# A graph layer with mixer and mixture of experts: a fifth node taken by maxima over all rows, a last slice of 123 steps, later scatters, and the last experts' weights issued behind the last fold

## The chip, the cores and the metric

The kernel runs on one core of one Trainium2 chip. The time is the device time of one execution in microseconds; the time of the kernel before is the median of three runs. One further execution was recorded by the hardware profiler, and every duration below is from that record. Differences of about 0.2% (2.4 us) are the smallest that these runs can tell from none.

## The reference

Cut to what matters here: `x` has 3125 rows (nodes, tokens) of 256 numbers, and there are 100000 edges `src -> dst`, sorted by `dst`, most of them into the lowest nodes.

```python
xn = layernorm(x)
# graph part: for each edge relu((xn[dst]-xn[src]) @ theta.T + xn[src] @ phi.T), maximum over the edges of a node
x = x + segment_max(relu(...), dst) + mixer(xn)          # a node without edges gets 0
xt = x; probs = softmax(layernorm(xt) @ Wr + br); top_p, top_idx = top_k(probs, 2)
h = gelu(einsum('end,edh->enh', xe, W1) + b1)            # 8 experts, 256 -> 1024 -> 256
x = x + sum over the two picked experts of weight * (h @ W2 + b2)
```

What an edge adds splits into a part of its source, `b = xn @ (phi - theta).T`, and a part of its destination; so a node needs only the maximum of `b` over its sources.

## The kernel before, in words

The nodes make 25 tiles of 128. The edges lie in reversed order of their destination over 128 partitions with 782 steps each: one step is one indirect gather on GpSimd (POOL, L107) that brings 128 rows of `b_d` into a window buffer (pool "g", five buffers of eight rows per partition), and one VectorE instruction `fold` (L366) that carries the running maximum along. Windows are stored to `s_d` through the SP queue (`move(nc.sync, ...)` in `folding`); the row at which a node's run ends is gathered from there again (`r`).

The steps are cut into four slices (`STEPS`), each of which completes a group of node tiles (`GROUPS`): tiles 12 to 24, then 5 to 11, then 1 to 4, then tile 0. When a slice is folded, its group follows: `carry` (L373 to L389) joins the partitions' maxima, `token_tile` (L425 on) makes the tokens and the router's logits, `dispatch` scatters the tokens' rows to `xs_d` by expert (POOL, L114), and `Stream.go` runs the experts over the rows in lots: load of rows, transposes (L698), scale `xe` (L709), first matmuls `hp` (L615), gelu (L617), second matmuls `yp` (L639), bias (L753), store to `ys_d`. An expert's 2 MB of weights come in four parts of 512 KB on ScalarE's DMA queue. Tile 0 is done by `dense_tile`: it goes through all eight experts in the order `DENSE` (5, 6, 7, 0, 1, 2, 3, 4) without routing, each with its own scaled input `xe` (L802, VectorE); three experts' weights are left from the stream, two (0 and 1) come in 1 MB halves by `dense_half`, three by `next_dense`. `combine` gathers the two expert rows of every token of the other tiles (POOL), weighs them on VectorE (L1308) and stores them to `out` (SP); it uses the window buffers.

The last 27 steps (`REST`) are never gathered. They hold edges into the nodes below `FIRST` = 4. For these `first_nodes` counts by one-hot matmuls which rows have an edge into which node and makes a mask `no_edge`, and `first_maxima` takes the maximum of all of `b` plus mask: 25 tiles times four nodes of VectorE instructions (L1228), spread at one per 1.4 ticks, then transposes (L1235), a reduction, two more transposes (L1242) and the result `first`, which tile 0 needs at L440. The last `KEPT` = 6 steps of slice 3 aren't stored: `pick_ends` (L1287) takes the ends in them from SBUF by one-hot matmuls that `last_ends` prepares.

The order of PE, VectorE, ScalarE and SP is written out by hand. Pieces of work are generators with a due time in ticks; a tick is one gather on POOL (about 1.25 us). `yield 8` in such a piece says that what follows is issued no earlier than 8 ticks on, and every engine's stream has just the order in which the pieces issued.

Of the kernel before, what the change touches and what calls it, by code (L numbers as in the profile page):

```python
# [8 lines left out]
F32 = mybir.dt.float32  # L9
# [5 lines left out]
OP = mybir.AluOpType  # L15
# [23 lines left out]


GROUPS = ((12, 25), (5, 12), (1, 5), (0, 1))
STEPS = (240, 195, 194, 126)
CAPS = (512, 256, 176)
LOT = (256, 256, 176)
G = len(GROUPS)
COL = [sum(STEPS[:g]) for g in range(G + 1)]


FIRST = 4
REST = T - COL[G]  # L50
W = 8
WN = 5
# [15 lines left out]
def gps_layer(ctx: ExitStack, tc: tile.TileContext, x, src, dst, thetaT, phiT, gbias, wq, wkvT,  # L68
# [583 lines left out]
    class Stream:  # L652
# [67 lines left out]
        def go(self):  # L720
            units = Units(self.ps, self.act)
            u, q = 0, -1
            for k in range(3):
                self.next_w(k)
                yield 25
            while True:
                if u == len(self.lots):

                    for _ in units.last():
                        yield room()  # L730
                    units.behind = None
                    if not self.open:
                        break
                    if G - 3 in self.through:
                        nc.scalar.activation(table, eps, AF.Sqrt)
                    while u == len(self.lots):
                        yield 1
                if ("xe", u) not in self.held:
                    self.rows(u // 2)
                    yield 8  # L740
                    self.turn(u)
                    yield 2
                    self.scaled(u)
                    yield 2
                g, e, h = self.lots[u]
                v = u // 2
                if u % 2 == 0:
                    ys = self.at(2) if v % 2 else self.act.tile([P, 4, D], F32, name="ys", bufs=1)

                def done(r, yp, u=u, ys=ys):  # L750
                    g, e, h = self.lots[u]
                    n = self.half(u)
                    nc.tensor.matmul(yp[0:n, :], ident[0:E, e:e + 1].to_broadcast([E, n]), b2_sb, start=False, stop=True)  # L753
                    nc.scalar.copy(ys[0:n, u % 2 * 2 + r, :], yp[0:n, :])
                    if u % 2 and r:
                        move(nc.scalar, self.two(ys_d, u // 2), self.as_two(ys, u // 2))
                        if u + 1 == len(self.lots) or self.lots[u + 1][0] != g:
                            self.through.add(g)

                between = {4: lambda: self.turn(u + 1), 6: lambda: self.scaled(u + 1)}  # L760
                if u % 2 == 0:
                    between[1] = lambda: self.rows(v + 1)
                if h == 0:
                    q += 1
                    if q:
                        between[7] = lambda: (self.next_w(q + 2, self.parts), self.part())
                at_step = dict(between)
                for f in (0, 2, 5):
                    between[f] = lambda f=f: (self.part(), at_step.get(f, int)())
                w1t, w2t = self.held["w", q]  # L770
                for _ in units.run(e, w1t, self.held["xe", u], w2t, done, between, 2, self.half(u)):
                    yield room()
                u += 1
            for k in range(3):
                dense_w[DENSE[k]] = self.held["w", q - 2 + k]
            dense_half(0, 1, xn_hi[:, 0:FC, :].rearrange("p i d -> p (i d)"), nc.scalar)
            clock["through"] = True

    def spread(pool, i, pick):
# [6 lines left out]
    def dense_tile(act, ps, mm, i, shared, w, next_w, order=range(E), ready=None):  # L786
# [5 lines left out]
        xT = act.tile([P, 2, P], F32, name="xT", bufs=1)  # L792
        nc.vector.tensor_copy(xT, tr)
        held = {}
        yield 1

        def scaled(k):
            if k < E:
                e = order[k]
                held["xe", e] = act.tile([P, 2, ROWS], F32, name="xe")  # L800
                for c in range(2):
                    nc.vector.tensor_scalar(held["xe", e][:, c, 0:P], xT[:, c, :], sm[:, c, e:e + 1],  # L802
                                            sm[:, 2 + c, e:e + 1], op0=OP.mult, op1=OP.add)

        while ready is not None and "through" not in ready:
            yield 1
        scaled(0)
        o = act.tile([P, D], F32, name="o", bufs=1)

        def second_bias():  # L810
# [156 lines left out]
    def first_nodes():  # L967
# [8 lines left out]
        nc.vector.tensor_scalar(high, high, lane, None, op0=OP.subtract)  # L976
        yield 1
        counts = no_edge.rearrange("p k i -> p (k i)")
        some = 7
        for t0 in range(0, REST, some):  # L980
            n = min(some, REST - t0)
            ones_of = []
# [125 lines left out]
    def dispatch(g, half, i0, i1, top, top_i, taken):  # L1108

        ro = at_hand["route"]  # L1110
        while not all(i in routed for i in range(i0, i1)) or len(taken) < half:
            yield 1
        yield 1
        made = []
        at = i0 - GROUPS[g][0]
        rest = shares(ro, i0, i1, top[:, at:at + i1 - i0, :], top_i[:, at:at + i1 - i0, :], made,
                      15 if g == G - 2 and half == 0 else 0)
        start(rest, clock["now"] + next(rest))
        yield from slots(ro, mm, g, half, i0, i1, made[0], taken)
        yield 1 if g == G - 2 else 9  # L1120
        put = []
        for i in range(i0, i1):
            n = rows_in(i)
            for k in range(2):
                put.append((xs_d[g][:], slot_i[0:n, k, i:i + 1], xn2(i)[0:n]))
        scatter(*put)

    def group(g):
# [42 lines left out]
            start(first_maxima())  # L1171
        if g == G - 2:
            clock["routed"] = True
            start(verdict())

    odd = keep.tile([1, 1], I32, name="odd")
# [30 lines left out]
    def first_maxima():  # L1207
# [11 lines left out]
        for i in range(NT):  # L1219
# [4 lines left out]
            for k in range(FIRST):  # L1224
# [4 lines left out]
                                                   op1=OP.max)  # L1229
                yield 1.4  # L1230
        most = at_hand["first"].tile([P, 2, FIRST], F32, name="most")
        for c in range(2):
            tr = mm.tile([P, FIRST, P], F32, name="mm")
            for k in range(FIRST):
                nc.tensor.transpose(tr[:, k, :], of_k[:, k, c * P:(c + 1) * P], ident)  # L1235
            on_pe(1.2)
            yield 4
            nc.vector.tensor_reduce(most[:, c, :], tr, AX.X, OP.max)
            yield 2
        rows_p = mm.tile([FIRST, 2, P], F32, name="mm")  # L1240
        for c in range(2):
            nc.tensor.transpose(rows_p[:, c, :], most[:, c, :], ident)  # L1242
# [2 lines left out]
        ends["first"] = at_hand["first"].tile([FIRST, D], F32, name="first")  # L1245
        nc.vector.tensor_copy(ends["first"], rows_p.rearrange("k c p -> k (c p)"))

        dense_half(0, 0, xn_lo[:, 1:1 + FC, :].rearrange("p i d -> p (i d)"))
        yield from last_ends()

    def end_ones(j):
        return xn_lo[:, SPLIT - KEPT // 2:SPLIT, :].rearrange("p i (c k) -> p (i c) k", k=P)[:, j, :]

    def last_ends():

# [59 lines left out]
    def combines(g):  # L1315

        i0, i1 = GROUPS[g]
        whole = i1 - (i1 == NT)
        for i in range(i0, whole, W // 2):
            nt = min(W // 2, whole - i)  # L1320
            start(combine(g, i, nt))
            yield 2 * nt
            if g == 0 and i == i0 + W // 2:

                while "shared" not in clock:
                    yield 1
                yield 6
                for k in range(2):
                    dense_half(1, k, wide.tile([P, HALF], F32, name="g"))
        if i1 == NT:  # L1330
            start(combine(g, NT - 1, 1))
            yield 2

    def finale():

        for g in range(G - 1):
            while g not in at_hand["ffn"].through:
                yield 1
            yield from combines(g)

    def starts(g):

# [7 lines left out]
    def folding():  # L1350

        for g in range(G):
            last = None
            rows = s_d[1 + P * COL[g]:1 + P * COL[g + 1], :].rearrange("(p t) d -> p t d", t=STEPS[g])
            for w, (t0, n) in enumerate(starts(g)):
# [6 lines left out]
                if g < G - 1 or t0 + n < STEPS[g]:  # L1362
                    move(nc.sync, rows[:, t0:t0 + n, :], wins[g, w][:, 0:n, :])
            clock["last"] = last
            if g == 0:
                open_late()
            start(group(g))
# [193 lines left out]
```

## Time and profile before

| | us |
|---|---|
| median of three runs (lowest, highest) | 1219.15 (1218.51, 1221.02) |
| the profiled execution | 1217.85 |
| its span, first to last instruction | 1216.0 |
| busy: TensorE, VectorE, ScalarE, POOL | 938.2, 678.6, 326.0, 885.8 |
| experts of group 0 on TensorE | 528 to 794 |
| experts of group 1 | 802 to 939.5 |
| experts of group 2 | 1007.8 to 1140.3 |
| last gather of an edge step (POOL) | 1114.62 |
| dense tile: first hp to the last o | 1140.36 to 1208.95 |

The mean granted TensorE clock of this execution is 0.856 of full speed. In the lines of the profile a row names the engine, the source line, the operation with the program's names (`out<-in`) and, in brackets, the engine's idle time before it with what ended it. In the table of stretches each row gives the busy time and the number of instructions of every engine, then the granted TensorE clock, the busy share of the DMA engines and the GB/s that they moved. In the chain of work that ended last, each row is a start, a duration and what ran or was waited for.

### The profile page before, as it was taken

The numbers are of one execution on the slowest core, as the hardware profiler recorded it, in microseconds if no ns is written. First come the engines' busy times: TensorE is split into PE (matmuls) and PEld (weight loads), VectorE is DVE, ScalarE is ACT, GpSimd is POOL, SyncE is SP. The second block draws the span as 40 slices with busy tenths as digits, with TensorE's granted clock in tenths as the row PEclk, the third lists the DMA queues.
The fourth block names the chain that finished last, engine by engine and source line by source line (L and its number), as shares of the span: only waits on it lengthen the run. The fifth ranks groups of instructions, "written<-read, shape, count | busy, mean of one in ns | idle before, by whom it ended". The sixth has DMA issues, their size and how long they took to land.

```text
span 1216.0 us, 13364 instructions
## 1 busy us (share of the span) xinstructions
PE 938.2 (77%) x3929; PEld 670.4 (55%) x3929; DVE 678.6 (56%) x1998; ACT 326.0 (27%) x762; POOL 885.8 (73%) x911
## 2 busy tenths in 40 slices
PE   6556866645923548689999999979999527999986
PEld 5323433323311323258888887868887315777786
DVE  7669866685336772433333587455546764433633
ACT  4212222210101222133333343323332112332331
POOL 6677777777777777777777777777777777776733
PEclk9778888866965557889999999989999557999998
DMA  8668877666685664467888787689999658998683
GB/s 280 214 200 277 302 253 242 227 227 207 207 292 194 239 235 157 156 238 258 285 307 310 251 284 271 227 308 356 380 370 367 219 191 305 375 387 301 201 338 94
DMA packets 103928, 320.13 MB, mean 263 GB/s; under 512 B 20897, under 2 KB 44186, under 8 KB 92325
## 3 DMA queue, kind: packets, MB, share of 16 engines
q0 software_dynamic: 44032, 119.73, 31.5%
q1 hardware_dynamic: 29724, 115.08, 24.4%
q10 hardware_dynamic: 30089, 84.36, 19.3%
q8 instruction: 33, 0.54, 0.2%
q14 instruction: 50, 0.41, 0.1%
HBM read 192.05 MB, written 127.04 MB: 262 GB/s over the span
## 4 chain that ended last, share of the span: by engine, by line
PE 43%; DMA 5%; issue 4%; POOL 3%; DVE 2%; ACT 1%; ACTq 0%; POOLq 0%; DVEq 0%; SPq 0%
PE yp L639 18%; PE hp L615 18%; PE yp L753 3%; POOL g L107 2%; DMA w<-in_w 2%; DMA g<-b_d,srcI 2%; PE trf L698 1%; POOL xs_d L114 1%; DMA xn_lo<-b_d 1%; PE am L445 1%; DVE g L366 1%; PE mm L491 0%; DMA xn_hi<-xs_d 0%; DMA r<-s_d,end_i 0%; PE mm L403 0%
## 5 line engine op out<-in xcount | busy, mean ns | idle before, releaser
L107 POOL DMA_INDIRECT g<-b_d,srcI x755 | 738.2, 978 | 238.4 <-issue 203.8
L366 DVE SCALAR_TENSOR_TENSOR g<-g,cut 128x256 f32<-128x256 f32 x751 | 363.5, 484 | 356.8 <-DMA g<-b_d,srcI 339.0
L639 PE MATMUL yp<-w,hT 128*128 128x256 f32 (+1 forms) x1120 | 296.8, 387 | 0.0
L615 PE MATMUL hp<-xe,w 128*128 128x256 f32 (+2 forms) x1216 | 285.9, 361 | 11.5 <-issue 5.6
L615 PEld LDWEIGHTS hp<-xe,w 128*128 128x128 f32 x1216 | 216.7, 196 | 49.2 <-issue 18.0
L617 ACT ACTIVATE hT<-hp,sm 128x256 f32<-128x256 f32 (+2 forms) x320 | 140.2, 439 | 335.8 <-PE hp L615 335.3
L639 PEld LDWEIGHTS yp<-w,hT 128*128 128x128 f32 (+1 forms) x1120 | 201.1, 185 | 39.7 <-issue 12.4
L1012 PE MATMUL kv<-wkv,xn_lo 128*128 128x512 f32 x96 | 54.5, 720 | 38.0 <-DVE kn L1030 24.1
L1012 PE MATMUL kv<-wkv,xn_hi 128*128 128x512 f32 x104 | 59.3, 724 | 30.9 <-DVE kn L1030 30.2
L107 POOL DMA_INDIRECT g<-ys_d,from_i x48 | 46.1, 960 | 32.4 <-DVE g L1308 18.7
L445 PE MATMUL am<-cr,oh 128*128 128x257 f32 x86 | 37.3, 560 | 27.8 <-DVE r L450 19.9
L1012 PEld LDWEIGHTS kv<-wkv,xn_lo 128*128 128x128 f32 x96 | 21.1, 231 | 63.8 <-issue 60.3
L1012 PEld LDWEIGHTS kv<-wkv,xn_hi 128*128 128x128 f32 x104 | 22.8, 230 | 58.3 <-issue 55.6
L1228 DVE SCALAR_TENSOR_TENSOR xn_lo<-xn_lo,no_edge 128x256 f32<-128x256 f32 x96 | 45.9, 479 | 16.1 <-DMA xn_lo<-b_d 16.1
L401 PE MATMUL mm<-bias,ones 1*128 1x512 f32 x50 | 32.4, 731 | 16.2 <-ACT x_sb L408 12.9
L753 PE MATMUL yp<-b_sb,ident 8*128 8x256 f32 (+1 forms) x128 | 43.9, 422 | 0.0
L1016 ACT ACTIVATE sq<-kv 128x1024 f32<-128x1024 f32 x25 | 25.5, 1019 | 59.3 <-PE kv L1012 59.3
L445 PEld LDWEIGHTS am<-cr,oh 128*128 128x128 f32 x86 | 20.3, 267 | 37.1 <-issue 24.9
L709 ACT ACTIVATE xe<-trf,sm 128x256 f32<-128x256 f32 (+1 forms) x64 | 31.3, 544 | 27.6 <-PE trf L698 27.6
L1035 PEld LDWEIGHTS dots_p<-kn,vn 128*128 128x128 f32 x200 | 26.9, 199 | 19.0 <-issue 19.0
L1024 ACT ACTIVATE rsk<-var,eps 128x16 f32<-128x16 f32 x25 | 7.7, 308 | 110.7 <-DVE var L1021 110.7
L698 PE MATMUL trf<-ident,xn_hi 128*128 128x128 f32 (+1 forms) x128 | 19.2, 275 | 22.2 <-DMA xn_hi<-xs_d 22.2
(285 smaller groups left out, 991.1 us busy)
## 6 DMA issues: line engine op xcount, KB each, us to landing
s_d<-g SPq DMA_DIRECT2D x80, 1024.0 KB
w<-in_w ACTq DMA_DIRECT2D x84, 512.0 KB
w<-in_w ACTq DMA_DIRECT2D x6, 2048.0 KB
g<-b_d,srcI POOLq DMA_INDIRECT x755, 4.5
s_d<-g SPq DMA_DIRECT2D x13, 896.0 KB
xn_hi<-xs_d ACTq DMA_DIRECT2D x12, 512.0 KB
xs_d<-zero ACTq DMA_DIRECT2D x8, 512.0 KB
b_d<-bt SPq DMA_DIRECT2D x5, 640.0 KB
```

The lines of the kernel that those rows point to most:

```text
L107: got = nc.gpsimd.indirect_dma_start(out=to, out_offset=None, in_=table, in_offset=row_index(index))
L366: nc.vector.scalar_tensor_tensor(g[:, j, :], last, cut[:, t:t + 1], g[:, j, :], op0=OP.add, op1=OP.max)
L401: nc.tensor.matmul(am, ones[0:1, :], bias, start=True, stop=False)
L445: nc.tensor.matmul(r2, picks[k], carried[g], start=(k == 0), stop=(k == len(slices) - 1))
L615: nc.tensor.matmul(hp[:, 0:n], w1t[:, c, f, :], xe[:, c, 0:n], start=(c == 0), stop=(c == 1))
L617: nc.scalar.activation(hT[f][:, 0:n], hp[:, 0:n], AF.Gelu, bias=sm[:, 4 + f, e:e + 1])
L639: nc.tensor.matmul(yp[r][0:part, :], hT[q][:, r * part:(r + 1) * part], w2t[:, q, :], start=(q == 0), stop=(q == FC - 1 and self.whole))
L698: nc.tensor.transpose(tr[:, c, r * n:(r + 1) * n], self.held["xs", u // 2][0:n, u % 2 * 2 + r, c * P:(c + 1) * P], ident[0:n, 0:n])
L709: nc.scalar.activation(xe[:, c, 0:n], self.held["tr", u][:, c, 0:n], AF.Identity, bias=sm[:, 2 + c, e:e + 1], scale=sm[:, c, e:e + 1])
L753: nc.tensor.matmul(yp[0:n, :], ident[0:E, e:e + 1].to_broadcast([E, n]), b2_sb, start=False, stop=True)
L1012: nc.tensor.matmul(kv[:, k, :], xnT(i, c), wkv[:, c, k * INNER:(k + 1) * INNER], start=(c == 0), stop=(c == 1))
L1228: nc.vector.scalar_tensor_tensor(of_k[:, k, :], b, no_edge[:, k, i:i + 1], of_k[:, k, :], op0=OP.add, op1=OP.max)
```

## The change

The last slice has 123 steps and not 126, so `REST` is 30 and `FIRST` 5: three gathers and folds fewer, 125 maxima for 100, a wider mask counted in five rounds for four. The scatters of groups 0 and 1 are issued 14 ticks and not 9 after the slots. When the experts of group 2 begin, the three pauses ahead of the first lot are 3, 1, 1 ticks and not 8, 2, 2. `first_maxima` waits 8 ticks between its last maximum and the transposes, which come in four batches for two; `last_ends` starts at group 2's routing and not behind `first_maxima`. The half of expert 0's weights that is loaded there goes to another place in `xn_lo`. The other half, and both halves of expert 1, are issued on SP's queue by the new `more_weights`, which starts behind the last fold; each begins with a memset of one column. Before, expert 1's two halves came in `combines` after its second tile group, a wait for "shared" (tile 0's weights of the picked experts) and 6 ticks, in which the other combines waited too; the half of expert 0 came on ScalarE's queue behind the whole stream of experts. The dense tile's first `xe` is issued once the last lot has begun, and no longer behind the stream's end.

```diff
-STEPS = (240, 195, 194, 126)
+STEPS = (240, 195, 194, 123)
-FIRST = 4
+FIRST = 5
...
                 if ("xe", u) not in self.held:
+                    soon = self.lots[u][0] == G - 2
                     self.rows(u // 2)
-                    yield 8
+                    yield 3 if soon else 8
                     self.turn(u)
-                    yield 2
+                    yield 1 if soon else 2
                     self.scaled(u)
-                    yield 2
+                    yield 1 if soon else 2
...
                 w1t, w2t = self.held["w", q]
+                if u + 1 == len(self.lots) and not self.open:
+                    clock["last lot"] = True
...
                 dense_w[DENSE[k]] = self.held["w", q - 2 + k]
-            dense_half(0, 1, xn_hi[:, 0:FC, :].rearrange("p i d -> p (i d)"), nc.scalar)
             clock["through"] = True
...
         held = {}
-        yield 1
...
+        if ready is not None:
+            while "last lot" not in ready:
+                yield 1
+        scaled(0)
+        yield 1
         while ready is not None and "through" not in ready:
             yield 1
-        scaled(0)
...
-        some = 7
+        some = 6
...
-        yield 1 if g == G - 2 else 9
+        yield 1 if g == G - 2 else 14
...
             clock["routed"] = True
+            start(last_ends())
             start(verdict())
...
         most = at_hand["first"].tile([P, 2, FIRST], F32, name="most")
+        yield 8
         for c in range(2):
-            tr = mm.tile([P, FIRST, P], F32, name="mm")
-            for k in range(FIRST):
-                nc.tensor.transpose(tr[:, k, :], of_k[:, k, c * P:(c + 1) * P], ident)
-            on_pe(1.2)
-            yield 4
-            nc.vector.tensor_reduce(most[:, c, :], tr, AX.X, OP.max)
-            yield 2
+            for k0, k1 in ((0, 3), (3, FIRST)):
+                tr = mm.tile([P, 3, P], F32, name="mm")
+                for k in range(k0, k1):
+                    nc.tensor.transpose(tr[:, k - k0, :], of_k[:, k, c * P:(c + 1) * P], ident)
+                on_pe(0.9)
+                yield 3
+                nc.vector.tensor_reduce(most[:, c, k0:k1], tr[:, 0:k1 - k0, :], AX.X, OP.max)
+                yield 1
...
-        dense_half(0, 0, xn_lo[:, 1:1 + FC, :].rearrange("p i d -> p (i d)"))
-        yield from last_ends()
+        dense_half(0, 0, xn_lo[:, SPLIT - FC:SPLIT, :].rearrange("p i d -> p (i d)"))
     def end_ones(j):
-        return xn_lo[:, SPLIT - KEPT // 2:SPLIT, :].rearrange("p i (c k) -> p (i c) k", k=P)[:, j, :]
+        return xn_lo[:, 1:1 + KEPT // 2, :].rearrange("p i (c k) -> p (i c) k", k=P)[:, j, :]
...
             start(combine(g, i, nt))
             yield 2 * nt
-            if g == 0 and i == i0 + W // 2:
-
-                while "shared" not in clock:
-                    yield 1
-                yield 6
-                for k in range(2):
-                    dense_half(1, k, wide.tile([P, HALF], F32, name="g"))
...
+    def more_weights():
+        for k in range(2):
+            to = wide.tile([P, HALF], F32, name="g")
+            nc.vector.memset(to[:, 0:1], 0.0)
+            dense_half(1, k, to)
+        while "last lot" not in clock:
+            yield 1
+        to = xn_hi[:, 0:FC, :].rearrange("p i d -> p (i d)")
+        nc.vector.memset(to[:, 0:1], 0.0)
+        dense_half(0, 1, to)
...
             clock["last"] = last
+            if g == G - 1:
+                start(more_weights(), clock["now"] + 1)
```

## The prediction

> **What bounds the kernel now.** I read the table of stretches first, to see where TensorE is the limit.
>
> ```profile
> core 0: us, PE busy (x) PEld busy (x) DVE busy (x) ACT busy (x) POOL busy (x), PEclk, DMA share, GB/s
> 940.00:1007.00 67.00, 24.76 (x74) 17.34 (x74) 46.30 (x186) 9.47 (x21) 50.81 (x53) 0.53 0.60 209
> 1007.00:1140.00 133.00, 125.12 (x630) 97.01 (x629) 58.66 (x155) 40.42 (x99) 97.67 (x102) 0.94 0.88 319
> 1140.00:1209.00 69.00, 61.79 (x389) 55.35 (x387) 30.68 (x77) 23.96 (x66) 31.88 (x33) 0.95 0.71 253
> ```
>
> From 940 to 1007 TensorE waits for group 2's gathers and routing (24.8 us busy of 67). Then come the experts of group 2 (1007 to 1140) and the dense tile 0 through all eight experts (1140 to 1209); in both TensorE is nearly full, so what the change can take is its waits there. The gathers that slice 3 loses run on POOL under the 125 busy microseconds: fewer of them are worth nothing by their count. Next the chain that ended last, for these two stages:
>
> ```profile
> 1016.36 6.92 DMA g<-b_d,srcI
> 1025.30 1.17 PE hp L615 x4
> ...
> 1081.21 15.02 DMA w<-in_w
> ...
> 1122.52 2.59 PE am L1287 x12
> ...
> 1181.96 5.55 issue
> 1187.52 1.19 PE hp L615 x4
> ```
>
> The two holes are seen in the timelines of TensorE (first four rows), VectorE and POOL:
>
> ```profile
> 1021.10 0.33 PE L1235 MATMUL mm<-ident,xn_lo 128*128 128x128 f32 x1 [1.66 <-DVE xn_lo L1228]
> 1024.82 0.48 PE L1235 MATMUL mm<-ident,xn_lo 128*128 128x128 f32 x1 [1.02 <-DVE xn_lo L1228]
> 1187.52 1.19 PE L615 MATMUL hp<-xe,w 128*128 128x128 f32 x4 [5.59 <-issue]
> 1192.69 0.61 PE L615 MATMUL hp<-xe,w 128*128 128x128 f32 x4
> ...
> 1186.15 0.48 DVE L1308 SCALAR_TENSOR_TENSOR g<-g,share,x_sb 128x256 f32<-128x256 f32 x1 [3.57 <-DMA g<-ys_d,from_i]
> 1187.08 0.60 DVE L802 TENSOR_SCALAR xe<-xT,sm 128x128 f32<-128x128 f32 x2
> ...
> 1182.22 0.94 POOL L107 DMA_INDIRECT g<-ys_d,from_i  x1 [6.81 <-DVE g L1308]
> 1183.46 0.95 POOL L107 DMA_INDIRECT g<-ys_d,from_i  x1 [0.30 <-issue]
> ```
>
> First hole: the transposes L1235 stand in TensorE's order before the last maxima L1228 are done. From 1019.44 to 1025.09 TensorE does nothing but four transposes (5.65 us), and until 1029.8 it runs at half speed. Second hole: the page calls it "issue", but the weights of that expert had landed at 1172.9. The input xe of the seventh expert (L802) stands in VectorE's order behind a combine's L1308, that behind gathers, and those on POOL behind an out store (issued 1164.66, landed 1181.5 while the DMA engines were 0.96 busy) that held the gathers' buffer.
>
> **The change, part by part.** The profiled execution took 1217.85 us (span 1216.0 and 1.85 around it), 1.3 under the median 1219.15; the sum is made on 1217.85 and shifted by 1.3.
>
> *Later scatters of groups 0 and 1.* Five ticks of 1.25 us, one per gather, is 6.25 us. POOL waited 1.77 us (747.15) and 1.17 us (774.99) ahead of two batches of scatters; less the usual 0.30 that is 2.3 us by which all later gathers run ahead, if the slots are then ready. The queue moved past is POOL's own, full of gathers, so nothing else is delayed. The experts of groups 0 and 1 start up to 6.25 us later and end near 946 instead of 939.5, under the 42 idle microseconds of 940 to 1007; if that cover were gone it would cost 6.25. Group 2's experts start 2.3 earlier (bounds 0 and 2.3).
>
> *Three steps fewer, five nodes.* 3 gathers at 1.25 us are 3.75 us on POOL. 25 more maxima at 0.479 us are 12.0 us of VectorE, which is 58.7 busy of 133 there. At 1.4 ticks each they take 35 ticks (44 us) more. Before, 88 maxima lay ahead of the pause at group 2's routing and 12 behind; now about 37 lie behind. With the 8-tick wait and the four batches of transposes (four ticks each, then four for rows_p) I count 52+8+16+4 = 80 ticks from the resumption, and slice 3 has (1114.62-995)/1.25 = 96 less 5. So "first" is copied just ahead of the last folds and no longer at 1046; its TensorE step must not come late in the expert stream, else the last folds queue behind its copy on VectorE. The counting with six steps a round (five rounds for four, seven ticks) lies in a stage with much idle TensorE time; 0.
>
> *The first hole.* The maxima are finished 8 ticks ahead of their transposes, and group 2's first lots are written 7 ticks earlier: 5.65 us go, and the half speed after (L615 groups at 1.38 us where full speed has 0.76), 3 us. VectorE's maxima may be up to 10 us late against the plan and still fit; bounds 5.65 and 8.65. The two added transposes cost 0.9.
>
> *Half speed after a short wait.* At 1096.36 TensorE had waited 1.99 us for weights, and L639 groups then took 1.6 us until 1100.7 against 1.03 at full speed. I therefore charge half speed to every wait of about 2 us. [...]
>
> *End of group 2's experts.* 1140.33 less 2.3 and 7.7 is 1130.3. Their weights come in 512 KB parts, 6 to 15 us each, with the DMA engines 0.88 busy, and an undisturbed lot takes 13.57 us; part of the gain may turn into waits for parts (as the 15.02 row). Whatever it is between 1130 and 1137, the next chain ends later.
>
> *Start of the dense tile.* It began at 1140.36, as the experts ended; its own chain had xe at 1139.0 to 1139.6. That chain runs from the picks L1287 (1122.36) over L439 (1126.77) to xe in 12.2 us. The last gather moves from 1114.62 by 2.3+3.75 = 6.05 us to 1108.6. But the picks stand behind some tail steps of the experts (about 1.45 us each) in TensorE's order, "first" comes just ahead of the last folds, and the last s_d store (5.7 us before) now shares its queue with 1 MB of expert 0. Of the 6.05 I take 3.2 (bounds 0 and 6.05): picks 1119.2, L439 1123.6, first dense step 12.9 later, 1136.5. That is 3.9 us (0 to 6.75).
>
> *The last experts' weights.* 1 MB each for expert 1's halves and expert 0's second half: issued 1146.63, 1147.35 and 1141.25, they now go out behind the last fold, into a stretch where 1117 to 1141 shows the DMA engines 0.36 busy at 109 GB/s. 3 MB move within some 14 us there, so the store of the first combines and the dense weights find a freer DMA. SP's queue: behind these three issues stand the out stores only. Each memset (0.06 us like L388) waits for its buffer; the folds whose windows held them are stored long before, 0. If the cover were missing (the r gather landing late), tile 0's chain pays, within the bounds above.
>
> *Combines without the pause.* About 6 ticks earlier in every order, and so also ahead of xe (L802) in VectorE's. The dense tile took 1208.95-1140.36 = 68.6 us, of which 5.59 wait, 2.6 half speed, 0.45 another wait at 1197.7: 60.0 unstalled. The fifth to seventh experts' xe now each stand behind a whole combine. With stores landing in 3 to 6 us (those at 1146.15, 1182.22 and 1191.81 took 5.8, 2.8 and 4.2) I expect waits of 1 and 2.3 and 2 of half speed: 5.3 for 8.6, a gain of 3.3 (bounds: gain 8.6, loss 16).
>
> *scaled(0) earlier, yields.* Within the chain already counted; 0 (0 to 0.5).
>
> Sum: 3.9+3.3 = 7.2, 1210.65 on the profiled execution, 1211.9 as a median. The first hole and the scatters, 10 us together, reach the end only through the 3.9.
>
> **The rivals.** *Everything goes:* picks 6.05 earlier (less what the chain was behind, 6.75 with 0.7 slack) and no dense waits: 6.75+8.6 = 15.3, 1203.9. For: the DMA gap is real. Against: three more combines in VectorE's order.
>
> *The gain ends at the next wait:* the dense tile starts as before or 1 us earlier, since "first" or the last store holds tile 0's chain, and its 8.6 us of waits stay, as the late weights had all landed in time before: 1218 to 1219. For: no weights were waited for in the dense tile.
>
> *Slower, VectorE's order:* the combines run ahead by 6 ticks, but gathers still wait for out stores #2 and #3, which took 11.7 and 16.8 us. Then xe of two late experts waits for gathers (5.6 and 2.6 half speed each, 16.4 for 8.6, +7.8 less 3.9 = +3.9, 1223); with three, 24.6, +12.1, 1231. It decides if a store lands later than about 4 us ahead of the step (gathers to L1308: 1182.22 to 1186.15), for the seventh expert later than 1174.
>
> *The change doesn't do what it says:* the 8 ticks are too few and the transposes wait for maxima again, at another place; 5 us of the hole stay, but the dense chain hides them: 1212 to 1215, within the forecast's range.
>
> **How the numbers follow.** Forecast 0.50, everything goes 0.15, gain swallowed 0.13, slower 0.22. About 0.2% (2.4 us) is what a measurement here can tell from no change. Faster: forecast and first rival, 0.65 and a little of the third, 0.67; same 0.12; slower 0.21. The forecast's own range is 1206 to 1216. For 8 in 10 it reaches to 1203.5 below and to the two-expert case above, 1223; the three-expert case is left out.
>
> **What would show it.** Right: no wait at L1235 over 0.5 us; experts of group 2 starting near 1005.5 and ended before 1137; first dense step near 1136.5; w12 halves landed before 1135; out stores under 8 us; dense tile near 65 us. Wrong: the dense tile's first step at 1140 or later; L1308 rows with waits over 3 us ahead of L802; TensorE waiting for L1242 or rows of weights over 2 us in 1007 to 1130.

## The result, and the profile after

The changed kernel took 1224.37 us (median of 20 runs, 1221.05 to 1233.6), the kernel before beside it 1220.72 (20 runs): ratio 1.0035, interval 1.0018 to 1.0052. It is slower by some 4 us where 7 us faster was forecast. A second measurement on one chip with later runs gave 1.0032 (1.0007 to 1.0058). The profiled execution of after took 1227.19 us, that of before 1217.85; single executions of one kernel differ by 10 us and more, so the 9 us between these two are not all the change. Four of the kernels timed below (the hole alone, before with earlier xe, the pause, and 1.12 ticks with earlier xe) were first run on a chip on which the kernel before itself took 1764.91 us, where the first has no ratio on record and the others had 0.994 (0.9861, 1.0018), 0.9984 (0.9937, 1.0031) and 0.9853 (0.9777, 0.993); only their repetitions elsewhere are used.

The table of stretches of the kernel after (columns as before):

```profile
940.00:1007.00 67.00, 29.14 (x104) 20.32 (x102) 45.04 (x183) 10.32 (x23) 48.82 (x50) 0.64 0.60 214
1007.00:1140.00 133.00, 120.98 (x617) 95.38 (x618) 64.91 (x166) 39.56 (x97) 92.49 (x95) 0.94 0.94 342
1140.00:1218.00 78.00, 67.55 (x405) 60.13 (x403) 34.12 (x98) 24.93 (x68) 37.78 (x39) 0.91 0.57 194
```

The middle stage has less TensorE time (120.98 for 125.12 us) although the hole at the transposes is gone, and the last stage is longer: the dense tile runs from 1145.01 to 1217.27, 72.3 us for 68.1. Its DMA share fell from 0.71 to 0.57, and that did not help it. The chain that ended last:

```profile
1114.41 5.24 DMA g<-b_d,srcI
1119.68 0.48 DVE g L366
...
1121.74 4.78 DMA s_d<-g
...
1127.25 6.88 DMA r<-s_d,end_i
...
1180.08 5.48 issue
...
1195.15 1.97 issue
```

Before, the chain lay on the experts of group 2; now it lies on the last gather, folds, store and row gather of tile 0. The experts end at 1141.9, and the dense tile starts 3.1 us later. The timeline of VectorE shows why the last store goes out at 1121.74 and not at 1113.53 as before:

```profile
1105.00 0.56 DVE L1246 TENSOR_REDUCE most<-mm 128x3 f32<-128x384 f32 x1 [9.93 <-PE mm L1243]
1110.70 0.43 DVE L1246 TENSOR_REDUCE most<-mm 128x2 f32<-128x256 f32 x1 [3.18 <-PE mm L1243]
1114.74 0.56 DVE L1246 TENSOR_REDUCE most<-mm 128x3 f32<-128x384 f32 x1 [1.66 <-PE mm L1243]
1119.34 0.42 DVE L1246 TENSOR_REDUCE most<-mm 128x2 f32<-128x256 f32 x1 [2.09 <-PE mm L1243]
1119.68 5.16 DVE L366 SCALAR_TENSOR_TENSOR g<-g,cut 128x256 f32<-128x256 f32 x10
```

TensorE waits for VectorE no longer; VectorE waits for TensorE, 9.93+3.18+1.66+2.09 = 16.9 us, and the last ten folds (some of whose rows had landed earlier) come after it in one block. In the dense tile the pattern of before is back twice (the timelines of POOL and VectorE, then TensorE's):

```profile
1172.00 0.94 POOL L107 DMA_INDIRECT g<-ys_d,from_i  x1 [10.19 <-DMA out<-g]
...
1178.65 0.48 DVE L1315 SCALAR_TENSOR_TENSOR g<-g,share,x_sb 128x256 f32<-128x256 f32 x1 [8.89 <-DMA g<-ys_d,from_i]
1184.71 0.48 DVE L1315 SCALAR_TENSOR_TENSOR g<-g,share 128x256 f32<-128x256 f32 x1 [1.46 <-DMA g<-ys_d,from_i]
1185.12 0.60 DVE L803 TENSOR_SCALAR xe<-xT,sm 128x128 f32<-128x128 f32 x2
```

```profile
1185.56 1.19 PE L615 MATMUL hp<-xe,w 128*128 128x128 f32 x4 [5.52 <-issue]
1197.12 1.19 PE L615 MATMUL hp<-xe,w 128*128 128x128 f32 x4 [2.01 <-issue]
```

The gathers of the combine of tiles 5 to 8 wait 10.19 us for an out store (issued 1161.55, landed 1171.24) that held their buffer, and then take 5.5 to 8.9 us each to land. The combine's L1315 (L1308 before) waits 8.89 us for the first of them, the xe of the sixth expert (L803, L802 before) stands behind four of its instructions, and TensorE behind xe. 12 us later it happens again at the seventh expert, whose xe stands behind gathers that began at 1186.56, when the next out store had landed (1185.79). Two other rows of after matter below, of POOL and of TensorE:

```profile
954.83 1.08 POOL L107 DMA_INDIRECT r<-s_d,end_i  x1 [3.44 <-DMA s_d<-g]
```

```profile
1096.25 0.93 PE L615 MATMUL hp<-xe,w 128*128 128x176 f32 x2 [4.53 <-DMA w<-in_w]
```

### The profile page after: what moved, and what is told of

The parts are those of the page before. It is cut to its first block, busy times and chain, and to the rows that moved or that the text cites. A ratio compares the mean times of both kernels' runs of the same rounds, so it can differ in the third digit from the quotient of the medians.

```text
span 1225.3 us, 13405 instructions
## 1 busy us (share of the span) xinstructions
PE 946.3 (77%) x3934; PEld 674.5 (55%) x3934; DVE 688.7 (56%) x2028; ACT 326.9 (27%) x762; POOL 886.1 (72%) x908
## 3 DMA queue, kind: packets, MB, share of 16 engines
q0 software_dynamic: 43888, 119.34, 30.6%
## 4 chain that ended last, share of the span: by engine, by line
PE 37%; DMA 27%; POOL 17%; issue 9%; DVE 8%; ACT 1%; POOLq 0%; DVEq 0%; SPq 0%; ACTq 0%
DMA g<-b_d,srcI 17%; PE hp L615 15%; POOL g L107 15%; PE yp L639 14%; DVE g L366 3%; DMA r<-s_d,end_i 3%; POOL xs_d L114 2%; PE yp L754 2%; DMA xn_lo<-b_d 2%; PE bp L241 2%; DMA w<-in_w 2%; PE trf L698 1%; DMA xn_hi<-xs_d 1%; PE am L445 1%; DMA ys_d<-xn_hi 1%
## 5 line engine op out<-in xcount | busy, mean ns | idle before, releaser
L615 PE MATMUL hp<-xe,w 128*128 128x256 f32 (+2 forms) x1216 | 290.1, 366 | 16.8 <-issue 7.5
L639 PE MATMUL yp<-w,hT 128*128 128x256 f32 (+1 forms) x1120 | 296.1, 386 | 0.0
L615 PEld LDWEIGHTS hp<-xe,w 128*128 128x128 f32 x1216 | 221.0, 200 | 54.9 <-issue 24.0
L639 PEld LDWEIGHTS yp<-w,hT 128*128 128x128 f32 (+1 forms) x1120 | 200.8, 185 | 39.7 <-issue 12.2
L1017 PE MATMUL kv<-wkv,xn_lo 128*128 128x512 f32 x96 | 51.6, 687 | 42.2 <-DVE kn L1035 28.3
L1234 DVE SCALAR_TENSOR_TENSOR xn_lo<-xn_lo,no_edge 128x256 f32<-128x256 f32 x120 | 57.5, 480 | 19.3 <-DMA xn_lo<-b_d 19.3
L107 POOL DMA_INDIRECT r<-s_d,end_i x25 | 24.8, 991 | 22.3 <-DMA s_d<-g 15.3
```

Of the source, the lines that this page charges most:

```text
L107: got = nc.gpsimd.indirect_dma_start(out=to, out_offset=None, in_=table, in_offset=row_index(index))
L615: nc.tensor.matmul(hp[:, 0:n], w1t[:, c, f, :], xe[:, c, 0:n], start=(c == 0), stop=(c == 1))
L639: nc.tensor.matmul(yp[r][0:part, :], hT[q][:, r * part:(r + 1) * part], w2t[:, q, :], start=(q == 0), stop=(q == FC - 1 and self.whole))
L1017: nc.tensor.matmul(kv[:, k, :], xnT(i, c), wkv[:, c, k * INNER:(k + 1) * INNER], start=(c == 0), stop=(c == 1))
L1234: nc.vector.scalar_tensor_tensor(of_k[:, k, :], b, no_edge[:, k, i:i + 1], of_k[:, k, :], op0=OP.add, op1=OP.max)
```

## The experiments

Each kernel was timed with the kernel before on the same chip (12 runs unless said). In the table "last gather" is the start of the last gather of an edge step, "chain" the time from there to the first dense step, "dense" from that to the start of the last o, all from each run's one profile.

| kernel | ratio to before (interval) | experts of group 2 | last gather | chain | dense |
|---|---|---|---|---|---|
| before | 1 | 132.6 | 1114.6 | 25.7 | 68.1 |
| after | 1.0035 (1.0018, 1.0052) | 130.4 | 1114.4 | 30.6 | 72.3 |
| after, again | 1.0032 (1.0007, 1.0058) | 128.9 | 1115.4 | 27.6 | 68.2 |
| after, scatters at 9 | 1.0045 (1.0015, 1.0074) | 125.6 | 1117.5 | 25.9 | 68.0 |
| after, four nodes | 1.0036 (1.0002, 1.0069) | 122.7 | 1119.8 | 23.0 | 75.5 |
| after, maxima at 1.12 | 1.0008 (0.9976, 1.0041) | 128.3 | 1114.0 | 27.2 | 68.6 |
| after, late weights and pause | 1.0002 (0.9970, 1.0035) | 127.3 | 1116.2 | 26.4 | 66.8 |
| after, pause | 0.9965 (0.9940, 0.9990) | 132.1 | 1111.8 | 32.2 | 67.5 |
| after, without late combines | 0.9940 (0.9915, 0.9966) | 129.0 | 1114.6 | 28.2 | 59.6 |
| before, hole alone | 0.9995 (0.9969, 1.0021) | 118.8 | 1126.5 | 23.4 | 67.3 |
| before, earlier xe | 0.9959 (0.9931, 0.9987) | 132.5 | 1120.1 | 23.7 | 64.5 |
| the same, again | 1.0001 (0.9976, 1.0026) | 131.2 | 1127.8 | 22.8 | 60.8 |
| after, 1.12, earlier xe | 0.9978 (0.9955, 1.0001) | 129.6 | 1117.3 | 28.6 | 66.5 |
| after, pause, earlier xe | 0.9971 (0.9946, 0.9995) | 127.2 | 1114.4 | 26.4 | 62.4 |
| the same at 1.12 | 0.9989 (0.9966, 1.0012) | 125.7 | 1117.0 | 26.5 | 61.1 |
| the same, 1.4, four nodes | 0.9963 (0.9934, 0.9992) | 129.3 | 1115.4 | 29.1 | 62.7 |

The theory from these rows: the pause that the diff takes out of the combines puts more of them ahead of the dense tile's xe on VectorE (E), and the reductions of the fifth node hold the last folds (B). Rivals: the later scatters (A), the early weights' load on the DMA (C), and chance.

**One part undone: the scatters.**

```diff
-        yield 1 if g == G - 2 else 14
+        yield 1 if g == G - 2 else 9
```

> The changed kernel with the scatters of groups 0 and 1 at 9 ticks again. Theory A (the later scatters push the experts of group 1 8 us on, so that their last weights and rows load the DMA while slice 2's last windows are stored; the row gather of group 2 then waits 3.4 us for those stores): that wait at 954.8 falls below 1 us, the experts of group 2 start at 1007 to 1009 for 1011.4. The time falls by 0 to 3 us only, because tile 0's chain is held by the reductions. Rival (the later scatters are harmless, group 2 is later by chance of POOL's pace): start of group 2's experts stays within 1 us of 1011.4, time within 1 us of the changed kernel.

The wait at the row gather is gone (0.31 us; it is 1.9 to 4.3 us in five of the eleven profiles with 14 ticks: after, its repetition and the kernels with the late weights, with the pause, and with pause and earlier xe), but the experts of group 2 began at 1014.6, later and not earlier, and the time is no better. Over the profiles with 9 ticks they begin at 1007.8, 1018.3, 1011.4, 1019.5 and 1014.6 (mean 1014.3), over the eleven with 14 ticks at 1007.4 to 1014.1 (mean 1011.0). So with the later scatters that stage begins some 3 us earlier on the mean, in spite of the new wait; with 12 us between single profiles the size is uncertain, and four of the five with 9 ticks also lack other parts of the change. What the later scatters take away shows on POOL: in the same five profiles its waits of over 1 us ahead of scatters (those of groups 0 and 1) add up to 2.9, 9.8, 0, 14.7 and 5.0 us, in the eleven others to 1.2 at most. The longest is in the repetition of before with earlier xe:

```profile
509.99 1.01 POOL L114 DMA_INDIRECT xs_d<-xn_hi,slot_i  x1 [10.47 <-issue]
```

Theory A falls as a loss; its rival, that the start stays within 1 us of 1011.4, missed too.

**The nodes, and the pace of the maxima.**

```diff
-STEPS = (240, 195, 194, 123)
-FIRST = 5
+STEPS = (240, 195, 194, 126)
+FIRST = 4
...
-        some = 6
+        some = 7
```

> The changed kernel with 126 steps in the last slice and four nodes by maxima, all else as changed. Theory B (25 more maxima at the same pace put the transposes and reductions of the maxima among the last lots of the experts; the reductions stand on VectorE ahead of the last folds and wait 16.9 us for TensorE): reductions come 40 to 45 us earlier, VectorE's waits for L1243 hold no fold that matters, the last stored window goes out by 1115 for 1121.7, the dense tile starts as the experts end, 1137 to 1140 for 1145.1; time 4 to 8 us below the changed kernel, so at or below the kernel before. Rival C (the 3 MB of late weights make the row gather and the stores of tile 0 late): dense start stays at 1143 or later, time within 2 us of the changed kernel.

```diff
-                yield 1.4
+                yield 1.12
```

> The changed kernel with the maxima at one per 1.12 ticks for 1.4, so that 125 take the 140 ticks that 100 took. Theory B: as many VectorE instructions as changed, but the reductions are done by 1080, the last window is stored by 1113, dense start 1136 to 1140; time 4 to 8 us below the changed kernel. Rival (12 us more of VectorE work is the loss, wherever it stands): time within 2 us of the changed kernel or above it.

The chain goes as theory B has it with four nodes: VectorE waits 2.3 us at the first reduction (1053.23) and at none after, and the chain is 23.0 us for 27.6 to 30.6. But three more gathers put the last one at 1119.8, the dense tile still starts at 1142.8, and it then took 75.5 us; the ratio is after's. The fifth node trades the last gather's start for the chain, and the end hardly sees it. At 1.12 ticks no reduction holds the folds either and the last store goes out at 1111.67, but the dense tile starts at 1141.3 and not at 1136 to 1140, and the ratio, 1.0008, overlaps after's. In neither kernel did theory B's 4 to 8 us come.

**The weights.** More_weights is taken out and the loads stand as before, with the pause in the combines:

```diff
-                start(more_weights(), clock["now"] + 1)
...
+            if g == 0 and i == i0 + W // 2:
+                while "shared" not in clock:
+                    yield 1
+                yield 6
+                for k in range(2):
+                    dense_half(1, k, wide.tile([P, HALF], F32, name="g"))
...
+            dense_half(0, 1, xn_hi[:, 0:FC, :].rearrange("p i d -> p (i d)"), nc.scalar)
             clock["through"] = True
```

> The changed kernel with the last experts' weights issued as before (expert 1 behind the second combine and the pause, the half of expert 0 behind the stream on ScalarE's queue). Theory B: the reductions still hold the last folds; only the row gather of tile 0 lands in 3 us for 6.9, so the dense tile starts 2 to 4 us earlier at 1141 to 1143, and its waits come to 6 to 9 us as before; time 0 to 4 us below the changed kernel. Rival C (the late weights are the whole loss): time 5 us or more below the changed kernel, dense start at 1140.

The row gather lands in time (L439 waits for nothing there, 1.92 us for it in after). The dense tile starts at 1142.5 and takes 66.8 us. The time is 0.58 us above before, 3 us better than after in difference to before, which is theory B's range and not rival C's. This edit undoes two things; the next undoes one.

**The pause alone.** As above without the weights: the loads stay early, the combines pause.

```diff
             yield 2 * nt
+            if g == 0 and i == i0 + W // 2:
+                while "shared" not in clock:
+                    yield 1
+                yield 6
```

> The changed kernel with the pause behind the second combine put back (without the weights, which stay early). Theory E: the later combines stand behind more of the dense tile's xe; the dense tile takes 65 to 69 us for 72.3, time 3 to 6 us below the changed kernel. Rival (the out stores' landing alone decides): dense tile within 2 us of 72, time within 2 us of the changed kernel.

The ratio is 0.9965, its interval wholly below after's. One wait of TensorE of over 1 us is left in the dense tile, on TensorE's timeline:

```profile
1190.43 0.98 PE L615 MATMUL hp<-xe,w 128*128 128x128 f32 x3 [5.39 <-issue]
```

What the pause orders can be counted in VectorE's timelines. The dense tile has 48 instructions of combines beside it. Ahead of the xe of the fifth to eighth expert stand 24, 30, 40 and 48 of them in the five profiles without the pause (after, again, scatters, four nodes, 1.12), 16, 26, 34 and 40 in three with it (late weights, pause, hole alone), and 20, 26, 36 and 44 in before. The combine of tiles 5 to 8, whose gathers wait for an out store, begins with the 27th. So without the pause the sixth expert waits, 5.3 to 6.5 us in all five; with it the sixth does not wait, and the wait of 1.7 to 5.6 us comes at the seventh. The out stores did not land sooner: with the pause the second and third took 17.1 and 15.3 us, in after 9.7 and 18.3. So the rival (their landing alone decides) falls, and the order is what counts.

The edit that the diff makes in passing, the pause taken from the combines, is what makes the change slow: of the parts undone one at a time (the scatters, the nodes with their steps, the pause) it is the only one whose return lowers the time clear of the intervals; the early weights were not taken out without the pause coming back. By medians against before that is some 6 us; the dense tiles of the profiles account for about half of it (below). The early weights, with the pause, do not harm; whether they help (0.9965 against 1.0002) the intervals leave open.

**Without the late combines.** The combines of tiles 20 to 23 and of groups 1 and 2 are left out, so 15 tiles are not written.

```diff
-        for i in range(i0, whole, W // 2):
+        for i in range(i0, min(whole, i0 + W) if g == 0 else i0, W // 2):
```

> The changed kernel without the combines of tiles 20 to 23 and 1 to 11 (their outputs are left out: 15 of 25 tiles unwritten), so that only two full combines and the last tile's stand in VectorE's order beside the dense tile. Theory E (combines ahead of xe and o on VectorE are the dense tile's waits): no wait of TensorE over 1 us after the third expert, dense tile 59 to 62 us, time 8 to 13 us below the changed kernel. Rival (weights that are loaded beside the experts hold it): dense tile 66 us or more.

10 runs: 1211.99 us, 11.7 below after on the same chip. The stretch of the dense tile:

```profile
1143.00:1203.00 60.00, 59.42 (x388) 54.72 (x387) 17.99 (x55) 23.63 (x65) 4.85 (x5) 0.97 0.41 140
```

TensorE is busy 59.42 of 60 us, with no wait for weights: with the late combines go all of the dense tile's waits. Since this also leaves out gathers and stores, it shows the size of the loss, not that the order on VectorE is its only way. The next kernels change that order alone.

**The inputs one expert earlier.**

```diff
-                held["xe", e] = act.tile([P, 2, ROWS], F32, name="xe")
+                if k % 2 == 0:
+                    held["two"] = act.tile([P, 2, ROWS], F32, name="xe")
+                held["xe", e] = held["two"][:, :, k % 2 * P:k % 2 * P + P]
...
         scaled(0)
+        scaled(1)
...
-            between = {1: lambda k=k: scaled(k + 1)}
+            between = {1: lambda k=k: scaled(k + 2)}
...
-                between[1] = lambda k=k: (next_w(k - 2), scaled(k + 1))
+                between[1] = lambda k=k: (next_w(k - 2), scaled(k + 2))
```

On the kernel before:

> The kernel before with each dense xe issued one expert earlier (two share a tile, so that three are at hand), all else as before. Theory E (the dense tile's waits are VectorE's order: xe behind a combine whose gathers wait for an out store): the wait of 5.59 us at the seventh expert goes or falls below 1.5 us, the dense tile takes 60 to 63 us for 68.1, time 4 to 8 us below the kernel before. Rival (the experts wait for their weights or the hT buffers all the same): dense tile 66 us or more, time within 2 us.

On the changed kernel at 1.12 ticks:

> The changed kernel with the maxima at 1.12 ticks and each dense xe issued one expert earlier. Theories B and E: last folds not held by the reductions, dense start 1138 to 1142, dense tile 60 to 63 us, time 8 to 12 us below the changed kernel and so 4 to 8 below the kernel before. Rival: dense tile 66 us or more and the time that of the kernel before.

On before, the wait of 5.59 us for xe is gone; what is left is a wait for o, which is also VectorE's and also behind the combines:

```profile
1197.16 0.70 PE L639 MATMUL yp<-w,hT 128*128 128x256 f32 x2 [3.19 <-DVE o L832]
```

The dense tile took 64.5 us, and 60.8 in the repetition, in which no wait over 0.9 us was left; but the repetition's ratio is 1.0001 for 0.9959. Its last gather began at 1127.8, 13 us later than in the profile of before. In that execution POOL had waited 10.47 us ahead of a scatter (the row above). So the shorter dense tile is shown on before, a shorter time only in one of two measurements. On the changed kernel at 1.12 ticks, without the pause, a wait of 4.43 us for o stays and the tile takes 66.5 us, as its rival had it: giving xe earlier is not enough where the combines also stand ahead of o.

**Both orders mended.** After with the pause and the earlier xe, then the same at 1.12 ticks, then at 1.4 with four nodes and 126 steps:

> The changed kernel with the pause put back and each dense xe issued one expert earlier. Theory E: of the one wait of 5.4 us that the pause left, xe no longer holds TensorE, but o on VectorE may; dense tile 62 to 66 us, time 5 to 9 us below the kernel before. Rival (both edits take away the same wait): time within 2 us of the kernel with the pause alone, 3 to 5 below the kernel before.

> As the one before, with the maxima at 1.12 ticks. Theory B (the reductions hold the last folds and the last store): 27 us and not 29 to 32 from the last gather to the first dense step; time 2 to 4 us below the kernel without that pace. Rival (TensorE's order holds the picks behind the experts' last steps, which wait for weights near 1095, so the earlier folds are worth nothing): the step from last fold to picks grows to 6 to 8 us and the time is within 2 us of the kernel without that pace.

> The changed kernel with four nodes and 126 steps, the pause put back and each dense xe issued one expert earlier; what is left of the change are the 8 ticks, the early experts of group 2, the later scatters and the early weights. By the three lengths of the runs so far: last gather 1118 to 1122, then 23 to 24 us (no reduction ahead of the last folds), then 61 to 63 us; time 4 to 8 us below the kernel before, within 2 us of the kernel before with the earlier xe alone. Rival (five nodes are worth the 5 us by which they bring the last gather forward): time 3 us or more above the five-node version, so at or above the kernel before.

With the first two ran the changed kernel once more, and with the third the kernel before with the earlier xe:

> The changed kernel once more, unaltered, beside the next three on one chip. The sum by three lengths that the runs so far give (last gather of an edge step; from it to the first dense step; from that to the last o): last gather 1112 to 1118, then 26 to 31 us, then 68 to 75 us; time 2 to 7 us above the kernel before. Rival (the first measurement was chance): within 2 us of the kernel before.

> The kernel before with each dense xe issued one expert earlier, once more, beside the run above: dense tile 62 to 65 us, time 3 to 6 us below the kernel before.

Pause and earlier xe: 1216.13 us, on the same chip as after's 1223.72 and before's 1220.37; dense tile 62.4 us. That is 4.2 us below before and no better than the pause alone (0.9971 and 0.9965), as the rival had it, although the dense tile is shorter (62.4 for 67.5). With 1.12 ticks 1218.01, no gain: the last fold ends at 1123.1, but the picks start at 1128.4, 5.3 us later, behind the experts' last steps in TensorE's order:

```profile
1125.71 2.82 PE L639 MATMUL yp<-w,hT 128*88 128x256 f32 x12
1128.37 2.75 PE L1297 MATMUL am<-g,xn_lo 128*128 128x256 f32 x12
```

So the reductions held the folds, but freeing those only uncovers the next row of the same chain. With four nodes 1217.35 (0.9963): five nodes show no gain at the end. The chain was 29.1 us there and not 23 to 24: the picks began at 1129.5, 7.7 us behind the last fold, with no reduction in the way. Over the five profiles in which the reductions are done long before the last folds the dense tile starts at 1143.6 on the mean, over the seven others of the changed kernel at 1143.1, so the reductions do not set its start. Three versions, then (the pause alone, pause with earlier xe, and that with four nodes), measured faster than both kernels, by 0.3 to 0.4% against before, with intervals that end just short of 1. Each was measured once on a chip of this speed, and before with earlier xe shows how far that carries: 0.9959, then 1.0001.

**The hole alone.** The kernel before with the 8 ticks and the 3, 1, 1:

```diff
-                    yield 8
+                    yield 3 if soon else 8
...
         most = at_hand["first"].tile([P, 2, FIRST], F32, name="most")
+        yield 8
```

> The kernel before with only the 8 ticks between the last maximum and the transposes and the 3, 1, 1 ticks for group 2's experts. The prediction's step: the 5.65 us of waits for L1228 and 3 us of half speed go and the experts of group 2 end 7 to 8 us earlier. Theory D (that stage is paced by the weights that the DMA brings, and tile 0's chain ends 0.5 us behind it): no wait at the maxima's transposes, but a wait of 3 to 5 us for weights near 1095 for 1.99; the experts take 126 to 129 us for 132.0 and TensorE then waits 3 us or more for tile 0's chain; time within 2 us of the kernel before. Rival (the hole reaches the end): time 4 us or more below the kernel before.

The experts of group 2 take 118.8 us for 132.6: the hole is gone, and more with it. The time is that of before. TensorE's timeline shows where it went, 1.09 us to weights and the rest to tile 0's chain:

```profile
1099.27 0.54 PE L615 MATMUL hp<-xe,w 128*128 128x176 f32 x2 [1.09 <-DMA w<-in_w]
...
1147.28 0.69 PE L482 MATMUL mm<-ident,xt 128*128 128x128 f32 x2 [5.94 <-ACT xt L471]
```

The experts end at 1137.0, the dense tile starts at 1149.8. The half of theory D that blames the weights does not show in this run (it began late, at 1018.3, after waits of 4.08, 1.78 and 3.9 us ahead of scatters); in the twelve other profiles without the hole the wait for weights between 1092 and 1100 is 2.1 to 6.1 us.

## Why the prediction was wrong

*The step that failed: "Combines without the pause", with "The last experts' weights" behind it.* It gave a gain of 3.3 us in the dense tile. Five profiles of the changed order (after, again, scatters, four nodes, 1.12) have 72.3, 68.2, 68.0, 75.5 and 68.6 us, mean 70.5; four with the pause and the old xe (before, hole alone, weights, pause) 68.1, 67.3, 66.8 and 67.5, mean 67.4: a loss of 3.1 where a gain was forecast. Most of it is in two of the five, but the profiled executions of the other three were 2.6 to 6.5 us faster than the medians of their kernels, that of after 2.8 slower, so single profiles give the size only roughly. The text named the row that decides (xe behind a whole combine) and then set against it that stores would land in 3 to 6 us, since 3 MB had moved out of their way. They did not: out store #3 took 18.3 us in after, 13.3 in the repetition, 19.2 with four nodes, 11.9 and 14.2 in the other two, against 16.8 before. What it shares the DMA with are the three 2 MB loads of `next_dense` (issued 1160.46, 1167.48 and 1174.59 in after, landing in 9.4 to 11.0 us; the DMA engines were 0.92 busy while store #3 ran), and these the change leaves in place. Nor were the stores all: the gathers behind store #2 took 5.5 to 8.9 us in after, and four more combine instructions than before stood ahead of each late xe, so the wait moved from the seventh expert to the sixth and could come twice. The stores of 2.8 to 5.8 us that the estimate was taken from were issued before those loads or after them; the nearest rows were the slow ones, 11.7 and 16.8.

*The rival "Slower, VectorE's order" came true in its mechanism*: in after two late experts wait, by 5.52 us (the sixth, behind out store #2) and 2.01 us (the seventh, behind store #3, which landed at 1185.8, far later than 1174). It was given 0.22. That its 1223 lies so near the measured 1224.37 is partly luck: it added 7.8 us in the dense tile and took off 3.9 for the earlier start, and the means of the profiles have 3.1 and 1.8.

*Start of the dense tile: right in sign, too large.* Kernels with before's front (before, earlier xe twice) start at 1140.4, 1143.8 and 1150.7, mean 1145.0; with after's front (after, again, pause, no late combines, pause with xe) at 1145.0, 1143.1, 1144.0, 1142.9 and 1140.8, mean 1143.2: 1.8 us for 3.9. The last gather moves from a mean of 1120.8 to 1114.1, 6.7 us for the 6.05 of the sum. The chain grows from 24.1 to 29.0, by 4.9 where 2.15 was allowed. The warning that "first" must not come late on TensorE was the right place: the four reductions ahead of it hold the folds already, and the row gather beside 3 MB of loads took 6.88 us for 2.8. But without either the dense tile started no earlier (1.12 ticks: row gather 2.8 us, start 1141.3; four nodes: 3.0 us, 1142.8); the picks then stand behind the experts' steps on TensorE. Which of these rows sets the start of the changed kernel is open.

*Later scatters:* right in direction. The last gather and the start of group 2's experts are forward on the mean (the start by 3.3 us, for 2.3), although a row gather now waits for stores in some executions. The 2.3 us were read from one execution, in which POOL waited 2.9 us ahead of scatters; in the five with 9 ticks it waited 0 to 14.7.

*The three lengths together* give -6.7+4.9+3.1, and 0.4 for the end (8.0 us from the last o to the span's end for 7.6): +1.7, against +3.65 measured. Of profiles that differ by 10 us in the last gather alone, no more can be asked.

*The first hole: right for its stage, worthless at the end,* as the text had it: 130.4 and 128.9 us of experts for 132.6, part of it turned into the weights' 4.53 us, the rest hidden by tile 0's chain. Its size was read too large: the three groups at half speed lose 1.9 us against full speed (1.38, 1.91 and 1.15 us for 0.76, 1.03 and 0.76), not 3, and of the 5.65 us the four transposes' own 1.75 stay.

*Half speed after a short wait:* held in some places, wrong as a charge on every wait. After the wait of 2.01 us at 1197.12 the L615 groups run at 1.19 and 1.06 us for 0.61, until 1200.6. After one of 3.19 us in before with earlier xe (the row at 1197.16 above) they run at full speed. The stretches behind these two waits, in after and in that kernel, give the granted clock as 0.54 and 1.00 (third number from the end):

```profile
1197.10:1200.80 3.70, 3.68 (x14) 3.40 (x15) 1.55 (x4) 0.73 (x2) 2.79 (x4) 0.54 0.67 213
1197.10:1201.00 3.90, 3.84 (x26) 3.61 (x27) 1.46 (x4) 1.10 (x3) 2.99 (x4) 1.00 0.39 113
```

It was 1.00 as well after waits of 2.10 us (four nodes, 1094.14), 2.16 (hole alone, 1203.55) and 2.55 (before with earlier xe, 1101.35); in the first and the last of these the L615 groups took 0.76 us and the L639 groups 1.03 behind the wait, as ahead of it. After the 1.99 us in before that the charge was read from it was 0.61 (1096.36 to 1100.70). So in these kernels a wait of about 2 us cost half speed in some places and nothing in others, and the charge was an estimate from one row.

## What to carry to other kernels

Where two streams share an engine in a fixed order, a pause that looks like lost time may be what keeps slow work behind urgent work (here 0.9965 of the time of before with it, 1.0035 without): look what stands behind each instruction before taking a wait out of its generator. Estimate a transfer's time from rows that ran beside the same neighbours, not from the mean of its kind (an out store of 512 KB took 16.8 and 18.3 us beside the 2 MB loads of before and after, the next of that size, issued behind them, 2.8 and 3.1). When a hole is closed in one stage, the next chain has to be shorter too; here hole, last folds, picks and the dense inputs each had only a few microseconds behind one another, and of what was tried only the order beside the dense tile reached the end.

## What the hardware showed that was not expected

One kernel's stages move between executions: with the same front the last gather of 755 began at 1114.6, 1120.1 and 1127.8. Most of the 13 us between the first and the third is one wait of POOL ahead of a scatter (10.47 us at 509.99), for which the profile names no cause. The gathers themselves vary less: the 240 of slice 0 took 0.988 us on average in before and 0.993 in after, which makes 1.2 us. The one wait is more than the whole change.

Among waits of 1.9 to 3.2 us on TensorE between the experts' matmuls, those of 1.99, 2.01, 2.03 and 2.99 us (before, 1096.36; after, 1197.12; pause, 1018.91; four nodes, 1205.90) were followed by some 4 us at a granted clock of 0.54 to 0.61, those of 2.10, 2.16, 2.55 and 3.19 us by one of 1.00. The length of the wait alone did not decide.
